# Cross-attention written as steps of one engine each, issued in the order of a table; PSUM as one tensor of three pairs and one of two banks; inverse roots on GpSimd

## The chip, the cores and the metric

One core of a Trainium2 chip runs the whole program as one launch. The metric is device microseconds of that core. The engines are TensorE (PE; its weight loads are listed apart as PEld), VectorE (DVE), ScalarE (ACT), GpSimd (POOL) and SyncE (SP), which here only issues DMAs. Each runs its own instruction queue in order; semaphores tie them together.

## What is computed

Eight batches of 112 tokens of width 256 go through two layers; a context of 375 tokens per batch is shared by both.

```python
# layer 0
n = layernorm(x)
q, k, v = n @ w_q + b_q, ctx @ w_k + b_k, ctx @ w_v + b_v   # 16 heads of 16
x = x + softmax(q k^T / 4) v @ w_out + b_out
n = layernorm(x)                                             # hyperbolic router:
h = project_to_ball(n @ Wp + bp)                             # distance to 8 centroids
x = x + sum over the top 2 experts of share * (gelu(n @ W1 + b1) @ W2 + b2)
# layer 1
n = layernorm(x)
x = x + softmax(q k^T / 4 + mask) v @ Wout                   # no biases, additive mask
n = layernorm(x)
x = x + bit_linear(silu(conv3(bit_linear(n, w1))), w2)       # ternary weights, 8-bit tokens
```

## The kernel before

**Stages.** The program is unrolled. Times are those of the profiled execution: start and first loads (0 to 21 us), attention 0 with the router and the quantisation of the last layer's weights mixed in (to 265), the end of the router (to 293), the experts over 21 tiles of 128 sorted rows with streamed weights (to 453), gathering the experts' rows back (to 474), attention 1 (to 690), the convolutional network (to 769).

**One batch of attention.** `attention()` (L492) holds the steps. `norm` (L529) applies the LN and transposes it (t_n). `query` (L541) makes q (t_q), scaled into two zero-padded copies, with the bias added on DVE in layer 0 (L553). `key` (L561) and `value` (L573) make K (t_k, evicted by ACT) and V (t_v; in layer 0 the bias is added on DVE, L581). `scores` (L587) computes four heads at a time into two PSUM tiles; DVE takes each row's maximum (L602; in layer 1 with the mask added, L608). `lower` (L613) splits the negated maxima in three bf16 parts and transposes them (t_top). `turned` (L627) computes the transposed scores with the maximum subtracted by a second product (L634, L641), in three steps of two tiles each; ACT takes exp (L657), in layer 1 after DVE has added the mask (L652). `weighted` (L663) is p times V (po). `finish_o` (L681), `finish_t` (L695) and `project` (L704) normalise, transpose (t_o, t_oT), project (t_out) and add to x, and take the next LN's statistics.

**Roots.** `ln_stats` (L214) and the router call `rsqrt` (L195): a bit trick and three Newton steps on DVE, ten DVE instructions for an LN's statistics with their bn_stats.

**PSUM.** Three pools: `ps_p` with three tiles of two banks (scores, transposed scores, keys, values), `ps_m` with one bank for all other products, `ps_o` with one bank for po and the router's small products.

**What sets the order.** Each step touches several engines. `add(slot, place, step, ...)` puts it in a plan, four slots to a batch, and L777 calls the steps sorted by slot and place. The Tile scheduler may then move instructions within each engine's queue. It adds the semaphore waits from the tiles that instructions read and write. `late()` (L887) clears the padded buffers and builds the convolution's tap matrices on POOL; it stands after attention 1 in the program, and the scheduler put it at 453 to 458, ahead of the first gathers.

**Loads.** SP issues x of all batches, then ctx of all batches, then wp, w1, w2, the masks and five expert tiles; ACT issues the small columns and layer 0's weights.

Of the kernel before, what the change touches and what calls it, by code (L numbers as in the profile page):

```python
# [21 lines left out]
SK = 375  # L22
# [25 lines left out]
for _name, _w in (("bq", 2), ("bk", 2), ("bp", 2), ("cw", NF * 3), ("cb", NF), ("cent", 2 * E)):  # L48
    COLS[_name] = (_n, _n + _w)
    _n += _w  # L50
NCOLS = _n

NWA, NWB = 2 * F + NF, NF * D + D


@with_exitstack
def xattn_ffn_kernel(
# [21 lines left out]
    xs = [const([S, D], f"x{b}") for b in range(B)]  # L79
    for b in range(B):  # L80
        nc.sync.dma_start(out=xs[b], in_=x_in[b])
    colt = const([128, NCOLS], "cols")
    nc.scalar.dma_start(out=colt, in_=cols)

# [8 lines left out]
    for name, src in (("q", wq0), ("k", wk0), ("v", wv0)):  # L93
        wts[0][name] = load_w(src, f"w{name}0", nc.scalar, f"w{name}")
    ctx_v = ctxT.rearrange("(c p) n -> p c n", p=128)
    ctx_t = []
    for b in range(B):
        t = const([128, 2, SK], f"ctx{b}")
        nc.sync.dma_start(out=t, in_=ctx_v[:, :, b * SK : (b + 1) * SK])
        ctx_t.append(t)  # L100
    rowt = const([128, 2 * D], "rows")
    nc.scalar.dma_start(out=rowt, in_=rows.partition_broadcast(128))
    wts[0]["o"] = load_w(wo0, "wo0", nc.scalar, "wo")
# [55 lines left out]
    topx = [const([S, G, 4, 32], f"top{i}", BF16) for i in range(2)]  # L159
    for t in topx:  # L160
        nc.gpsimd.memset(t, 0.0)
# [5 lines left out]
    nc.gpsimd.memset(minus_magic, -MAGIC)  # L167
    desc = const([128, E], "desc")
# [45 lines left out]
    def ln_stats(b):  # L214

        st = sp.tile([S, 6], F32, tag="bnst", name="bnst")
        nc.vector.bn_stats(st, xs[b])
        mv = sp.tile([S, 2], F32, tag=f"mv{b}", name="mv")
        nc.vector.bn_aggr(mv, st)
        nc.vector.tensor_scalar_add(mv[:, 1:2], mv[:, 1:2], 1e-5)  # L220
        rs = sp.tile([S, 1], F32, tag=f"rs{b}", name="rs")
        rsqrt(mv[:, 1:2], rs, 1, "ln")
        return mv, rs

# [5 lines left out]
    kv = [[None] * B, [None] * B]  # L230
    made = [0]

    def key_buf(layer, b):
        kv[layer][b] = [kp.tile([128, 2, SK], F32, tag="k", name="k"), vbuf[made[0] % 3]]
        made[0] += 1

    def key_products(layer, b, g, t):
        for c in range(2):
            nc.tensor.matmul(  # L239
                t, wts[layer]["k"][:, c, g * 128 : (g + 1) * 128], ctx_t[b][:, c, :],  # L240
                start=(c == 0), stop=(c == 1),
            )

    def value_products(layer, b, i, t):
        for c in range(2):
            nc.tensor.matmul(  # L246
                t, ctx_t[b][:, c, i * KC : (i + 1) * KC], wts[layer]["v"][:, c, :],
                start=(c == 0), stop=(c == 1),
            )
# [5 lines left out]

    class Router:
        def __init__(self, pool, misc, small):
            self.pool, self.misc, self.small = pool, misc, small
            self.cproj = const([128, 2, E], "cproj")
            self.cn = const([128, E], "cn")  # L260
            self.cn1 = const([128, E], "cn1")
# [4 lines left out]
        def ball_scale(self, sq, r, n, name):  # L266

            c = self.tmp(f"c{name}", n, sq.shape[0])
            nc.vector.tensor_scalar_max(c, sq, 1e-14)
            rsqrt(c, r, n, f"ball{name}")  # L270
            nc.vector.tensor_scalar(r, r, 0.95, 1.0, ALU.mult, ALU.min)

        def centroids(self):

            cent = col("cent", 0, 2 * E).rearrange("p (c e) -> p c e", c=2)
            csq = self.pool.tile([128, 2, E], F32, tag="r_csq", name="csq")
            nc.vector.tensor_mul(csq, cent, cent)
            t = self.small("t_c")[:, :E]
            for c in range(2):
                nc.tensor.matmul(t, ones, csq[:, c, :], start=(c == 0), stop=(c == 1))  # L280
            nc.vector.tensor_copy(self.cn, t)
            cs = self.tmp("cs", E, 128)
            self.ball_scale(self.cn, cs, E, "c")
            nc.vector.tensor_mul(self.cproj, cent, cs.unsqueeze(1).to_broadcast([128, 2, E]))
            nc.vector.tensor_mul(self.cn, self.cn, cs)
            nc.vector.tensor_mul(self.cn, self.cn, cs)
            nc.vector.tensor_scalar_min(self.cn, self.cn, 0.99)
            nc.vector.tensor_scalar(self.cn1, self.cn, -1.0, 1.0, ALU.mult, ALU.add)

        def norm(self, b, stats):  # L290
            n = self.pool.tile([S, D], F32, tag="r_n", name="rn")
            ln_apply(n, b, stats)
            return n

        def turn(self, n):
            t = self.misc("t_rn")[:, : 2 * S].rearrange("p (c s) -> p c s", c=2)
            for c in range(2):
                nc.tensor.transpose(t[:, c, :], n[:, c * 128 : (c + 1) * 128], ident[:S, :S])
            nT = self.pool.tile([128, 2, S], F32, tag="r_nT", name="rnT")
            nc.scalar.copy(nT, t)  # L300
            return nT

        def hyper(self, nT):
            t = self.misc("t_xh")[:, : 2 * S].rearrange("p (c s) -> p c s", c=2)
            for o in range(2):
                for c in range(2):
                    nc.tensor.matmul(
                        t[:, o, :], wp_t[:, c, o * 128 : (o + 1) * 128], nT[:, c, :],
                        start=(c == 0), stop=(c == 1),
                    )  # L310
            xh = self.pool.tile([128, 2, S], F32, tag="r_xh", name="xh")
            xsq = self.pool.tile([128, 2, S], F32, tag="r_xsq", name="xsq")
            for o in range(2):
                nc.scalar.activation(xh[:, o, :], t[:, o, :], AF.Identity, bias=col("bp", o))
                nc.scalar.activation(xsq[:, o, :], t[:, o, :], AF.Square, bias=col("bp", o))
            return xh, xsq

        def centre(self, xh, xsq):

            tmp = self.tmp  # L320
            t = self.small("t_g")[:S, : E + 1]
            for c in range(2):
                nc.tensor.matmul(t[:, 0:E], xh[:, c, :], self.cproj[:, c, :], start=(c == 0), stop=(c == 1))
            for c in range(2):
                nc.tensor.matmul(t[:, E : E + 1], xsq[:, c, :], ones[:, 0:1], start=(c == 0), stop=(c == 1))
            g, r = tmp("g", E + 1), tmp("r", 1)
            nc.vector.tensor_copy(g, t)
            self.ball_scale(g[:, E : E + 1], r, 1, "x")
            return g, r

        def distance(self, g, r):

            tmp = self.tmp
            xn = tmp("xn", 1)
            nc.vector.scalar_tensor_tensor(xn, g[:, E : E + 1], r, r, ALU.mult, ALU.mult)
            nc.vector.tensor_scalar_min(xn, xn, 0.99)
            xn1 = tmp("xn1", 1)
            nc.vector.tensor_scalar(xn1, xn, -1.0, 1.0, ALU.mult, ALU.add)
            m2r = tmp("m2r", 1)
            nc.vector.tensor_scalar_mul(m2r, r, -2.0)  # L340

            dif = tmp("dif", E)
            nc.vector.scalar_tensor_tensor(dif, g[:, 0:E], m2r, self.cn[:S], ALU.mult, ALU.add)
            nc.vector.tensor_scalar(dif, dif, xn, 0.0, ALU.add, ALU.max)

            den = tmp("den", E)
            nc.vector.tensor_scalar(den, self.cn1[:S], xn1, 1e-7, ALU.mult, ALU.add)
            nc.vector.reciprocal(den, den)
            nc.vector.scalar_tensor_tensor(dif, dif, 2.0, den, ALU.mult, ALU.mult)
            nc.vector.tensor_scalar(dif, dif, 1.0, 1.0 + 1e-7, ALU.add, ALU.max)  # L350
            v = tmp("v", E)
            nc.vector.tensor_scalar_mul(v, dif, -1.0)
            return v

        def pick(self, v, m, k):

            oh, f = self.tmp(f"oh{k}", E), self.tmp("f", 1)
            nc.vector.tensor_reduce(m[:, k : k + 1], v, AX.X, ALU.max)
            nc.vector.scalar_tensor_tensor(oh, v, m[:, k : k + 1], desc[:S], ALU.is_equal, ALU.mult)
            nc.vector.tensor_reduce(f, oh, AX.X, ALU.max)  # L360
            nc.vector.tensor_scalar(oh, oh, f, None, ALU.is_equal)
            if k == 0:
                nc.vector.scalar_tensor_tensor(v, oh, -1e30, v, ALU.mult, ALU.add)
# [128 lines left out]
    def attention(layer, stats, stats_next):  # L492
        res = None
        with (
# [284 lines left out]
            if layer == 0:  # L779
                res = rt.further()  # L780
# [368 lines left out]
```

## Time and profile before

| what | us |
|---|---|
| times of three runs | 766.53, 777.14, 777.37 (median 777.14) |
| the profiled execution: its time, its span | 771.0, 769.3 |
| mean granted clock of PE in it | 0.872 |
| first scores of attention 0 | 21.31 |
| last output product of attention 0 | 264.35 |
| first expert product | 292.96 |
| first scores of attention 1 | 474.25 |
| last output product of attention 1 | 688.07 |

The profile gives, for each instruction, engine, start and duration; a group is all instructions of one line with the same operands, and "idle before" is the time in which that engine stood before them, with what ended it. The granted clock is PE's clock as a share of full speed. A steady period (from one batch's step to the same step of the next batch) is about 30 us in attention 0 and 27.0 us in attention 1.

### The profile page before, as it was taken

How to read it: one execution, taken by the hardware profiler on the slowest of the kernel's cores; microseconds unless marked ns; L12 is line 12 of the kernel's file. 1: busy time of each engine (PE TensorE's matmuls, PEld its weight loads, DVE VectorE, ACT ScalarE, POOL GpSimd, SP SyncE). 2: the span in 40 equal slices, each digit the busy share in tenths (PEclk: the TensorE clock that was granted, in tenths of full speed). 3: DMA queues.
4: the chain of work that ended last, by engine and by line, in shares of the span. 5: the costliest groups of instructions: out<-in, count | busy, mean ns of one | idle time of the engine just before them, and what ended most of it. 6: DMA issues, size and time to landing. Idle time of an engine off the chain costs nothing.

```text
span 769.3 us, 14093 instructions
## 1 busy us (share of the span) xinstructions
PE 652.8 (85%) x5498; PEld 476.9 (62%) x5498; DVE 415.1 (54%) x1638; ACT 244.6 (32%) x480; POOL 55.8 (7%) x103
## 2 busy tenths in 40 slices
PE   4899889898898738999999984988888888979994
PEld 2455556575566527999889962555555545558883
DVE  6956684856845571011111108777568666775763
ACT  1023332233225203433333420143423332345430
POOL 4000000000000110000000038000000000000000
PEclk9989995988859857999999995589999987879996
DMA  9999101000000103997889902000000000000000
GB/s 297 363 345 350 64 3 60 9 13 29 27 13 8 32 22 128 344 338 279 319 310 355 360 28 78 7 2 1 1 2 2 1 1 2 1 1 1 13 13 24
DMA packets 37070, 81.63 MB, mean 106 GB/s; under 512 B 3228, under 2 KB 30220, under 8 KB 31628
## 3 DMA queue, kind: packets, MB, share of 16 engines
q1 hardware_dynamic: 34092, 75.72, 27.8%
q0 software_dynamic: 1536, 3.67, 1.6%
q10 hardware_dynamic: 1376, 1.34, 0.6%
q8 instruction: 43, 0.70, 0.4%
q14 instruction: 23, 0.19, 0.1%
HBM read 60.54 MB, written 20.19 MB: 105 GB/s over the span
## 4 chain that ended last, share of the span: by engine, by line
PE 39%; DVE 15%; DMA 3%; issue 3%; ACT 1%; POOL 1%; POOLq 0%; DVEq 0%; SPq 0%; ACTq 0%
PE t_h L842 10%; PE t_y L853 9%; PE t_c L1000 4%; DVE sm L608 3%; DVE pT L652 3%; PE sc L597 2%; PE t_v L246 2%; PE t_k L239 2%; PE t_p L634 2%; DMA we<-in_WA_dram 2%; PE po L675 2%; PE t_q L546 1%; PE t_y L1051 1%; DVE a L208 1%; DVE ys L1043 1%
## 5 line engine op out<-in xcount | busy, mean ns | idle before, releaser
L597 PE MATMUL sc<-k,q 32*112 32x375 f32 x512 | 105.1, 599 | 26.5 <-DVE pT L652 15.0
L842 PE MATMUL t_h<-tnT,we 128*128 128x128 f32 x672 | 91.9, 281 | 2.2 <-DMA we<-in_WA_dram 1.9
L842 PEld LDWEIGHTS t_h<-tnT,we 128*128 128x128 f32 x672 | 87.4, 194 | 9.4 <-DVE y L855 2.7
L846 ACT ACTIVATE hT<-t_h,we 128x128 f32<-128x128 f32 x168 | 61.4, 367 | 93.0 <-PE t_h L842 87.5
L634 PE MATMUL t_p<-q,k 32*125 32x224 f32 x768 | 82.0, 426 | 1.2 <-DVE top L602 0.4
L853 PE MATMUL t_y<-we,hT 128*128 128x256 f32 x336 | 82.8, 380 | 0.0
L608 DVE CUSTOM_DVE_ANT_0 sm<-sc,mask 112x375 f32<-112x375 f32 x128 | 62.6, 543 | 34.0 <-PE sc L597 34.0
L602 DVE TENSOR_REDUCE top<-sc 112x2 f32<-112x750 f32 x64 | 58.7, 933 | 32.1 <-PE sc L597 32.0
L657 ACT ACTIVATE pT<-t_p 125x896 f32<-125x896 f32 x48 | 41.4, 914 | 100.1 <-PE t_p L641 100.1
L597 PEld LDWEIGHTS sc<-k,q 32*112 32x112 f32 x512 | 33.9, 198 | 58.5 <-DVE pT L652 25.6
L853 PEld LDWEIGHTS t_y<-we,hT 128*128 128x128 f32 x336 | 59.1, 191 | 5.5
L652 DVE TENSOR_TENSOR pT<-t_p,mask 125x896 f32<-125x896 f32 x48 | 50.1, 1085 | 22.1 <-PE t_p L641 13.7
L657 ACT ACTIVATE pT<-pT 125x896 f32<-125x896 f32 x48 | 45.6, 950 | 51.2 <-DVE pT L652 50.1
L239 PE MATMUL t_k<-ctx,wk 128*128 128x375 f32 x128 | 52.9, 560 | 8.0 <-DMA ctx<-in_ctxT_dram 7.5
L634 PEld LDWEIGHTS t_p<-q,k 32*125 32x125 f32 x768 | 44.9, 209 | 17.4 <-issue 6.1
L675 PE MATMUL po<-pT,v 125*32 125x112 f32 x1536 | 51.5, 283 | 2.7 <-ACT pT L657 2.7
L675 PEld LDWEIGHTS po<-pT,v 125*32 125x32 f32 x1536 | 39.9, 119 | 20.9 <-issue 11.9
L246 PE MATMUL t_v<-wv,ctx 128*125 128x256 f32 x192 | 50.7, 413 | 1.2 <-DVE top L602 1.2
L831 DVE COPY tnT<-t_tn 128x256 f32<-128x256 f32 x21 | 8.9, 425 | 79.0 <-PE t_tn L829 72.5
L855 DVE TENSOR_TENSOR y<-t_y,we 128x256 f32<-128x256 f32 x21 | 8.9, 425 | 68.9 <-PE t_y L853 67.1
L246 PEld LDWEIGHTS t_v<-wv,ctx 128*125 128x125 f32 x192 | 37.8, 205 | 10.2 <-DVE top L602 2.0
L239 PEld LDWEIGHTS t_k<-ctx,wk 128*128 128x128 f32 x128 | 26.7, 222 | 27.3 <-issue 14.4
(214 smaller groups left out, 860.6 us busy)
## 6 DMA issues: line engine op xcount, KB each, us to landing
we<-in_WB_dram SPq DMA_DIRECT2D x21, 1152.0 KB, 7.5
we<-in_WA_dram SPq DMA_DIRECT2D x21, 1028.0 KB, 5.6
tok<-zero SPq DMA_DIRECT2D x8, 896.0 KB, 9.8
ysc<-zero SPq DMA_DIRECT2D x8, 896.0 KB, 10.3
ctx<-in_ctxT_dram SPq DMA_DIRECT2D x8, 375.0 KB, 6.4
tn<-tok SPq DMA_DIRECT2D x21, 128.0 KB, 6.8
ysc<-y SPq DMA_DIRECT2D x21, 128.0 KB, 3.2
we<-in_w1T_dram SPq DMA_DIRECT2D x1, 1024.0 KB, 10.0
```

The costliest lines, as they stand in the source:

```text
L239: nc.tensor.matmul(t, wts[layer]["k"][:, c, g * 128 : (g + 1) * 128], ctx_t[b][:, c, :], start=(c == 0), stop=(c == 1),)
L246: nc.tensor.matmul(t, ctx_t[b][:, c, i * KC : (i + 1) * KC], wts[layer]["v"][:, c, :], start=(c == 0), stop=(c == 1),)
L597: nc.tensor.matmul(ts[j // 2][:S, j % 2, :SK], q[r, c, i, :], k[r, c, :], start=True, stop=True)
L602: nc.vector.tensor_reduce(top[:, g, 2 * m : 2 * m + 2], ts[m][:S, :, :SK], AX.X, ALU.max, negate=True)
L608: nc.vector.tensor_tensor_reduce(out=sm, in0=ts[m][:S, n, :SK], in1=mask_t, scale=-1.0, scalar=3.0e38, op0=ALU.add, op1=ALU.min, accum_out ...
L634: nc.tensor.matmul(ts[j // 2][:KC, j % 2, n * 2 * S : (n + 1) * 2 * S], k[r, c, i * KC : (i + 1) * KC], q[r, c].rearrange("p i s -> p (i s)"),
L652: nc.vector.tensor_tensor(pT, src, mask2[:, lo : lo + 4 * S].unsqueeze(1).to_broadcast([KC, 2, 4 * S]), ALU.add,)
L657: nc.scalar.activation(pT, src, AF.Exp)
L675: nc.tensor.matmul(po[32 * j : 32 * j + 32, g, :], v[:, i, h, :], st[b][f"pT{s}"][r // 2][:, r % 2, lo : lo + S], start=(i == 0), stop=(i ...
L842: nc.tensor.matmul(ph[:, i, :], w1[:, c, f * 128 : (f + 1) * 128], nt[:, c, :], start=(c == 0), stop=(c == 1),)
L846: nc.scalar.activation(hT[:, f, :], ph[:, i, :], AF.Gelu, bias=b1[:, f : f + 1])
L853: nc.tensor.matmul(py, hT[:, f, :], w2[:, f, :], start=(f == 0), stop=(f == NF - 1))
```

## The change

**Steps.** Each step is now what one engine does: the first letter of its name is the engine (P, D, A, G for POOL, S for SP). The main ones: `Pk0, Pk1` and `Pv0..2` (halves of K, thirds of V), their evictions `Aka0, Aka1, Ava0..2`; `Ptn, AnT, Ptq, Aq0, Aq1`; `Ps0..3` with two maxima each (`Dm00` to `Dm31`); `Dsp0..4, Ptt, Alow` (the split maxima); `Pp0..2` with `Da..` (mask, layer 1) and `Ae..` (exp); `Pw0, Pw1` (p times V) with `Au0, Au1`; `Pto, Drc, Do, Pot, AoT, Pout, Dx`; `Dbn, Dba, Grt, Dn` (LN; the names with 2 are those of the next LN). In layer 0 also `Drn, Ptrn, ArnT, Ptxh, Axh, Ptg, Drg, ..., Prank, Drow, ..., Gsc` (router), `Dta..Dtf` (quantisation; `Dtb0` is the second half of the sum over w1), and `PX..` (layer 1's keys and values of batches 0 and 1).

**Order.** `ORDER` gives each step a time, in batches; the step of batch b stands at b + time, and all are issued in the order of these times under a manual schedule, so that nothing is moved within PE, DVE, ACT and POOL.

**PSUM.** One tile `pairs` of three pairs of banks, taken in turn by `Ps` and `Pp`; one tile `banks` of two banks, taken in turn by everything else, K and V among it.

**Engines.** The LN's root, the ball's root and the share's root are `pow` on POOL. q and V are evicted by ACT. The values' bias, which softmax weights that sum to one carry through unchanged, is multiplied by w_out once and added to the output bias. Centroids are normalised once at the start.

**Loads and late work.** wk0 is the first load of the ACT queue, x and ctx of each batch follow one another on SP; the fifth expert tile's load waits for the end of the quantisation of w2. The tap matrices are built one at a time in layer 1 (`Glt0..7`). The experts' and the convolution's code is unchanged.

The core of the diff:

```diff
+ORDER = [
+    [
+        ("Dtb0", -9.7742, 2, 2), ("Dbn", -3.0611, 0, 7), ("Dba", -2.6269, 0, 7), ("Dta0", -1.9080, 2, 2),
+        ("Grt", -1.5529, 0, 7), ("Dta1", -0.9759, 4, 4), ("Dn", -0.6930, 0, 7), ("Ptn", -0.4046, 0, 7),
+        ("AnT", -0.3659, 0, 7), ("Pk0", -0.3527, 0, 7), ("Aka0", -0.2457, 0, 7), ("Ptq", -0.2253, 0, 7),
...
+        ("Ava2", 0.3755, 0, 7), ("Ps0", 0.5977, 0, 7), ("Dm00", 0.6331, 0, 7), ("Dm01", 0.7107, 0, 7),
+        ("Ps1", 0.7235, 0, 7), ("Dm10", 0.7948, 0, 7), ("Sld", 0.9531, 7, 7), ("Dm11", 1.0045, 0, 7),
...
+        ("Dte0", 1.7855, 3, 3), ("Alow", 1.7987, 0, 7), ("Pp0", 1.9159, 0, 7), ("Ae00", 1.9480, 0, 7),
+        ("Ae01", 2.0936, 0, 7), ("Dbv", 2.0991, 0, 0), ("Pp1", 2.2561, 0, 7), ("Ae10", 2.2881, 0, 7),
...
+            pairs = ps.tile([128, 3, 2, 512], F32, tag="pairs", name="pairs")
+            banks = ps.tile([128, 2, 512], F32, tag="banks", name="banks")
+            turn_of = {"pair": 0, "misc": 0}
+
+            def pair(name):
+                turn_of["pair"] += 1
+                return pairs[:, turn_of["pair"] % 3]
+
+            def misc(name):
+                turn_of["misc"] += 1
+                return banks[:, turn_of["misc"] % 2]
...
+                @step(f"Grt{mark}")
+                def _(b, i=i):
+                    rs = sp.tile([S, 1], F32, tag=f"rs{b}", name="rs")
+                    mv = st[b].pop("mv")
+                    nc.gpsimd.tensor_scalar_add(rs, mv[:, 1:2], 1e-5)
+                    nc.gpsimd.tensor_tensor(rs, rs, minus_half[:S, :1], ALU.pow)
...
+            for g in range(G):
+                @step(f"Ps{g}")
+                def _(b, g=g):
+                    q, k = st[b]["q"], kv[layer][b]["k"]
+                    c, i = g // 2, g % 2
+                    st[b][f"s{g}"] = ts = [pair("sc"), pair("sc")]
...
+            plan = sorted((b + t, i, b, n) for i, (n, t, b0, b1) in enumerate(ORDER[layer]) for b in range(b0, b1 + 1))
+            with tc.manual_schedule(engines={ET.PE, ET.DVE, ET.Activation, ET.Pool}):
+                for _, _, b, n in plan:
+                    do[n](b)
```

## The prediction

> **What bounds the kernel now.** I read the page's busy shares and slices first, then busy time by stage, then groups by line, then single rows around the waits.
>
> ```profile
> PE 652.8 (85%) x5498; PEld 476.9 (62%) x5498; DVE 415.1 (54%) x1638; ACT 244.6 (32%) x480; POOL 55.8 (7%) x103
> PEclk9989995988859857999999995589999987879996
> ```
>
> TensorE is busy 85% of the span, and its clock falls now and then. By stage (window, its length, then busy us of PE, PEld, DVE, ACT, POOL, granted clock, DMA share, GB/s):
>
> ```profile
> 21.00:265.00 244.00, 218.32 (x2110) 142.63 (x2110) 157.62 (x646) 73.09 (x131) 15.10 (x17) 0.86 0.29 99
> 265.00:293.00 28.00, 8.76 (x39) 7.09 (x37) 18.78 (x149) 2.24 (x6) 3.77 (x4) 0.57 0.15 45
> 293.00:453.00 160.00, 157.99 (x1046) 144.95 (x1046) 16.84 (x40) 62.71 (x169) 0.00 (x0) 0.99 0.79 291
> 453.00:474.00 21.00, 8.09 (x31) 5.75 (x30) 10.86 (x45) 2.17 (x4) 17.20 (x21) 0.75 0.23 67
> 474.00:690.00 216.00, 187.62 (x1882) 113.81 (x1883) 151.09 (x544) 73.68 (x107) 6.95 (x9) 0.83 0.01 4
> 690.00:769.30 79.30, 62.49 (x361) 55.95 (x359) 45.13 (x101) 28.02 (x60) 3.37 (x6) 0.89 0.04 12
> ```
>
> PE is 89% busy in attention 0 and 87% in attention 1: it bounds both, and DVE has a third of each stage to spare. So work taken off DVE is worth little by itself. What counts is whether PE still finds its next operands and banks ready. The readers of PSUM that release it, and the one wait that costs most in attention 1:
>
> ```profile
> L602 DVE TENSOR_REDUCE top<-sc 112x2 f32<-112x750 f32 x64 | 58.7, 933 | 32.1 <-PE sc L597 32.0
> L657 ACT ACTIVATE pT<-t_p 125x896 f32<-125x896 f32 x48 | 41.4, 914 | 100.1 <-PE t_p L641 100.1
> L608 DVE CUSTOM_DVE_ANT_0 sm<-sc,mask 112x375 f32<-112x375 f32 x128 | 62.6, 543 | 34.0 <-PE sc L597 34.0
> L652 DVE TENSOR_TENSOR pT<-t_p,mask 125x896 f32<-125x896 f32 x48 | 50.1, 1085 | 22.1 <-PE t_p L641 13.7
> ```
>
> ```profile
> 534.68 0.89 PE L597 MATMUL sc<-k,q 32*112 32x375 f32 x4
> 537.75 0.89 PE L597 MATMUL sc<-k,q 32*112 32x375 f32 x4 [2.19 <-DVE pT L652]
> 538.57 2.47 PE L675 MATMUL po<-pT,v 125*32 125x112 f32 x48
> ```
>
> In the second fence PE stands for 2.19 us, and the next step, po, takes 2.47 us where it takes 1.36 at full clock: the slices by half a microsecond show half clock from 538.5 to 542. A hole of 2 us is paid twice.
>
> **The change, part by part.** The order of the compiled program, with its waits, gives more than the diff. `pairs` (six banks) and `banks` (two) are each ONE tensor now, and each access of such a tensor waits for the access before it in program order on another engine, whichever bank that touched. In layer 0 the exp of pair 0 (Ae01) waits for the scores of Ps2, issued after its own products into other banks; the maximum Dm11 of one pair waits for Ae00 of another; Ps1 waits for Dm01, whose pair it does not write. Au0 waits for Ptt, Alow for Ptq, Dx for Ptn, Pv1 for Ava0, Pv2 for AoT. Before, every tile of its pool was a tensor of its own and had only its own readers. So there are two chains per batch, each strictly in the table's order, instead of rings of three and two. I walk one steady period of each layer through these waits, engines in order.
>
> Durations at full clock, from the rows: Ps 0.89, Pp 1.63 (three steps 4.9), Pk 1.40 and Pv 0.95 (t_k 2.79, t_v 2.85 a batch), Pw 1.36, Ptq and Pout 1.12, Ptxh 1.04, Ptg 1.0, Pto 0.65, other transposes 0.4, Prank 0.6; Ae 0.91, Aka 0.57 (layer 0) and 0.43, Ava 0.37, Axh 1.44 (four of 0.36), Aq 0.72 (layer 0), the other ACT copies 0.35 to 0.53; Dm 0.93 in layer 0 and 2x0.54 in layer 1, Da 1.085, Drc and Do 0.25 and 0.42, Dn, Dc, Dbn, Dx 0.42, small DVE operations 0.15 to 0.25. A hop between engines is 0.05, from these rows (DVE ends 470.54, PE starts 470.60 and ends 471.23, ACT starts 471.27):
>
> ```profile
> 470.14 0.40 DVE L227 TENSOR_SCALAR n<-x,mv,rs 112x256 f32<-112x256 f32 x1
> 470.60 0.63 PE L536 MATMUL t_n<-ident,n 112*128 112x112 f32 x2 [11.67 <-DVE n L227]
> 471.27 0.35 ACT L538 COPY nT<-t_n 128x224 f32<-128x224 f32 x1 [11.51 <-PE t_n L536]
> ```
>
> Layer 0, ends of steps from the start of Pp0: Pp0 1.63, Ae00 2.60, Dm11 3.59, Drow 3.76, Ptrn 4.23, ArnT 4.64, Pk1 6.10, Pto 6.75, Aka1 7.38, Ps2 7.64, Ptxh 8.68, Axh 10.18, Drc and Do 10.91, Dm20 (behind them on DVE) 12.00, Pp1 13.69, Ae10 14.66, Dm21 15.65, Ps3 16.60, Ae11 17.57, Dm30 and Dm31 19.66, Pp2 21.35, Pout and Ptn 22.88, Ps0 23.77, Ae21 24.74, AnT 25.09, Pk0 26.55, Pw0 27.91, Ps1 28.80, Ptt 29.16, Au0 29.57, Ptq 30.75, Alow 31.34, Pw1 32.76, then Pp0 again: 33.0 with what is carried over. PE's own bill is 24.0 of it, and it has holes of 1.6, 2.3 and 1.4 us. Period before: 30.
>
> Layer 1, from the start of Ps3: Dm30 and Dm31 3.13, Pp2 4.82, Pk0 6.22, Pv1 7.17, Aka0 7.66, Pot 8.13, Ps0 9.02, Da21 10.17, Dc0 and Dm00 11.68, Ps1 12.63, Dm01 and Dm10 14.87, Pp0 16.56, Dm11, Da00 and Da01 20.07, Ps2 21.02, Pw1 22.38, Pp1 24.01, Dm21, Da10 and Da11 27.34: 27.4. PE's bill is 20.9, the largest hole 2.0. Period before: 27.0.
>
> Half clock on top: I price a hole of over a microsecond at one stretch of 3.5 us like that from 538.5. It loses half its progress over the part of the path that is PE's (16 of 33 us, 12.6 of 27.4; more inside a stretch, where PE's steps are the longer ones: about 0.65), so 1.1 us. Layer 0: three, 3.5 us. Layer 1: the one of 2.0 and a share of five holes of 0.5 to 0.9: 1.8. Bounds: nothing, and half of PE's path at half clock (+8 and +6). Taken: periods 36.5 and 29.2, near the lower bound as the 2.19 us row is.
>
> The sum, against 771.0 (span 769.3; the median shown is 777.1, so I am 6 us under it from the start). Attention 0 lasts 243.0 from first scores (21.31) to its last output product (264.35), 8.1 periods; eight of 36.5 are 292: +49. Attention 1 lasts 213.8, 7.9 periods; eight of 29.2 are 234: +20.
>
> Start: +23. DVE meets the half-sum Dtb0 of w1 before any LN, and w1 lands at 23.1 (issued 13.07, 10.0 to landing). Then Dtb0 1.2, statistics of two batches, a root and Dn: 27.4. Then one chain through `banks`, PE cold as at 12.16 (t_k 4.83): Ptn, AnT 28.7, Pk0, Aka0 32.2, Ptq, Aq 35.8, Pk1, Aka1 38.5, three Pv with their copies 43.5: first scores at 44 instead of 21.3. Bounds +12 (full clock at once) and +26.
>
> Combine, 453 to first scores at 474.25: -9. Taps (3.18) and the hpad memsets (1.3) no longer lead the gathers on POOL; ten DVE operations of an LN become two on DVE; DVE operations of 1.4 and 2.3 us beside POOL work go. Bounds -12, 0.
>
> Roots on POOL (two operations, between a 88 ns memset and an 833 ns tap): hidden by 2 us of slack behind Dba2 in layer 0 and 4 in layer 1; beyond that DVE waits in Drn. DVE loses some 55 us of LN roots, 27 of ball and z roots, 10 of values' bias and 7 of q (24 of 417 ns, 16 of 444): nothing, DVE's time on the path is the maxima, masks and splits, which stay. ACT gains 24 evictions and 32 quarter-q's: they are in the walk. The folded bias (two operations and a product) once: under 2 us. The first loads change places (wk0 first, x and ctx in turns): 0, since the first scores wait for DVE by then. MoE, router tail and FFN: unchanged code, 0, bounds -2 and +4 for the fifth expert load, now behind Dtf1.
>
> 771 + 49 + 20 + 23 - 9 = **854**.
>
> Two rules beside this. The Trainium skill's "PSUM — Partial Sum Buffer", section "PSUM bank collisions raise a hardware error", asks for a guard by bank; by it these chains would not be needed, and the sum would be the first rival's 712. The compiled waits decide. Its "TensorE: Matmul & The Clock Gate", part 1, lets the clock drop after a window of about 3.4 us idle; the 2.19 us row shows a drop after less. By the rule no hole of the walk costs clock, and the sum is 811.
>
> **The rivals.** *The rings hold after all (the other side)*: if waits on other banks' accesses are always met before they matter, PE runs its bill of 24.0 and 20.9 a batch with 11 and 14 us of hops, fill and drain, 203 and 181 us of attention: 771 - 40 - 33 + 14 - 9 - 3 (tail, shorter root chains on DVE) + 12 (the half clock left) = 712. Against it: in the walk such waits end last at some 30 places a period; it decides from periods of 28.5 and 26 (-15 - 6 + 14 - 9 = -16). *No more half clock*: periods 33 and 27.4, 264 and 219: 771 + 21 + 5 + 23 - 9 = 811. For: before ran at 0.86 and 0.83 with holes too. *Clock falls for most of a period*: 41 and 33, 328 and 264: 771 + 85 + 50 + 25 - 9 = 922. For: 115.5 to 136 was half clock with PE busy 18.92 of 20.50 us. *The walk is too strict*: fill and drain are shorter than eight periods and DVE's fewer operations close holes: periods 31 and 27, 248 and 216, start +12: 771 + 5 + 2 + 12 - 9 = 781.
>
> **How the numbers follow.** Chances: the walk with clock 0.42, full clock 0.25, low clock 0.16, too strict 0.11, rings 0.06. Range 780 to 915: from the too-strict case to just under the low-clock case. Faster by over 2% (which is what a measurement here can tell) only with the rings: 0.05. Within 2%: most of the too-strict case, 0.09. Slower: 0.86.
>
> **What would show it.** Right: first scores after 40; maxima and exps of layer 0 that each start just after the other's end, with PE idle before Pk1, Pp1 and Pk0; DVE busy near 105 and 124 us in the two attentions and yet longer stages; PE under 80% busy in both, clock under 0.86 and 0.83. Wrong: PE at 87% or more, periods under 29 and 26. Start, combine and each attention can be read apart.

## The result, and the profile after

The changed kernel takes 816.15 us (median of four runs, 812.27 to 818.54), the kernel before 777.25 (766.53 to 781.77): a ratio of 1.0531, interval 1.0431 to 1.063. Ratios here are of fast runs alone, since some executions of one and the same kernel take some 2% longer at a lower granted clock. The forecast was 854 in a range of 780 to 915. The profiled execution has a span of 816.8 us against 769.3, and its stages show where the 47.5 us arose (ends of stages read from the timeline: first scores, last output product, first expert product, first scores, last output product, end):

| stage | before | after | difference | forecast |
|---|---|---|---|---|
| start to first scores | 21.3 | 46.8 | +25.5 | +23 |
| attention 0 | 244.1 | 265.7 | +21.6 | +49 |
| rest of the router | 27.6 | 40.8 | +13.2 | 0 |
| experts and gathers | 181.3 | 173.3 | -8.0 | -9 |
| attention 1 | 215.9 | 211.2 | -4.7 | +20 |
| convolutional network | 79.2 | 79.0 | -0.2 | 0 |

The busy shares, TensorE's slices and its clock, of the changed kernel:

```profile
PE 621.6 (76%) x5502; PEld 454.3 (56%) x5502; DVE 351.1 (43%) x1096; ACT 269.1 (33%) x576; POOL 95.3 (12%) x185
PE   0587877777777676679999999467777777678994
PEclk9999899979987695879999999668999999788997
```

PE's share fell from 85% to 76%, although the clock is no lower. DVE has 64 us less to do and the kernel is 39 us slower at the median: DVE did not bound it. The two attentions by busy time, with the columns of the windows before:

```profile
46.82:312.48 265.66, 198.63 (x2073) 126.52 (x2072) 113.74 (x369) 91.77 (x185) 32.75 (x50) 0.87 0.16 52
526.62:737.84 211.22, 157.34 (x1902) 98.39 (x1902) 142.36 (x424) 75.12 (x134) 26.96 (x45) 0.90 0.02 7
```

No engine is busy more than 75% of either stage. That is the mark of waits, and the groups by line name them. The maxima of layer 0, the scores, and the exp:

```profile
L796 DVE TENSOR_REDUCE topf<-pairs 112x2 f32<-112x750 f32 x64 | 59.3, 935 | 107.8 <-ACT pT L869 70.8
L786 PE MATMUL pairs<-k,q 32*112 32x375 f32 x512 | 66.6, 594 | 33.8 <-DVE pT L857 18.1
L869 ACT ACTIVATE pT<-pairs 125x896 f32<-125x896 f32 x48 | 43.9, 920 | 68.3 <-PE pairs L846 34.5
```

Before, the maxima stood 32.1 us in front of this line, all of it for scores, which are their data. Now DVE stands 107.8 us, of which 70.8 for an exp on ACT. A maximum uses nothing of an exp: it waits because the exp touched another pair of the same tensor just before it in the program. In the timeline, around one Pp0 of attention 0:

```profile
223.28 0.66 PE L839 MATMUL pairs<-q,k 32*125 32x224 f32 x8
225.17 0.36 PE L454 MATMUL banks<-ind,below 112*112 112x8 f32 x2 [0.65 <-ACT q L728]
227.02 0.41 PE L334 MATMUL banks<-ident,rn 112*128 112x112 f32 x2 [1.29 <-DVE row L461]
227.87 2.51 PE L740 MATMUL banks<-ctx,wk 128*128 128x375 f32 x4 [0.44 <-ACT rnT L339]
235.39 2.04 PE L760 MATMUL banks<-wv,ctx 128*125 128x256 f32 x4 [2.02 <-DVE dif L420]
```

```profile
224.99 0.94 ACT L869 ACTIVATE pT<-pairs 125x896 f32<-125x896 f32 x1
```

```profile
225.96 0.94 DVE L796 TENSOR_REDUCE topf<-pairs 112x2 f32<-112x750 f32 x1 [4.75 <-ACT pT L869]
226.81 0.15 DVE L461 TENSOR_TENSOR row<-banks,first 112x8 f32<-112x8 f32 x1
```

Read across the engines: Ae00 ends at 225.93 and Dm11 starts at 225.96, Drow follows it on DVE and ends at 226.96, Ptrn starts on PE at 227.02. These are the walk's links in the walk's order, 0.03 to 0.06 us apart, with the holes where the walk had them (1.29 for the 1.6 before Ptrn, 2.02 for the 2.3 before Pv0). Pk1, at 227.87, takes 2.51 us instead of the walk's 1.40: it fell into a stretch at half clock.

### The profile page after: what moved, and what is told of

Same layout as the page of the kernel before. It is cut to its first block, busy times and chain, and to the rows that moved or that the text cites. A ratio compares the mean times of both kernels' runs of the same rounds, so it can differ in the third digit from the quotient of the medians.

```text
span 816.8 us, 13738 instructions
## 1 busy us (share of the span) xinstructions
PE 621.6 (76%) x5502; PEld 454.3 (56%) x5502; DVE 351.1 (43%) x1096; ACT 269.1 (33%) x576; POOL 95.3 (12%) x185
## 4 chain that ended last, share of the span: by engine, by line
PE 61%; DVE 20%; ACT 8%; DMA 6%; issue 4%; POOL 1%; ACTq 0%; SPq 0%; POOLq 0%; DVEq 0%
PE t_h L1049 9%; PE t_y L1060 8%; PE pairs L786 8%; PE pairs L839 6%; PE banks L740 5%; DVE pT L857 5%; DVE sm L802 5%; PE banks L884 4%; DVE topf L796 4%; PE t_c L1204 4%; ACT pT L869 3%; PE banks L760 3%; PE banks L933 2%; DMA tok<-rn,at 2%; PE banks L713 1%
## 5 line engine op out<-in xcount | busy, mean ns | idle before, releaser
L796 DVE TENSOR_REDUCE topf<-pairs 112x2 f32<-112x750 f32 x64 | 59.3, 935 | 107.8 <-ACT pT L869 70.8
L786 PE MATMUL pairs<-k,q 32*112 32x375 f32 x512 | 66.6, 594 | 33.8 <-DVE pT L857 18.1
L839 PE MATMUL pairs<-q,k 32*125 32x224 f32 x768 | 62.8, 417 | 25.6 <-DVE topf L802 13.0
L802 DVE CUSTOM_DVE_ANT_0 sm<-pairs,mask 112x375 f32<-112x375 f32 x128 | 63.7, 544 | 39.7 <-PE pairs L786 27.9
L740 PE MATMUL banks<-ctx,wk 128*128 128x375 f32 x128 | 62.5, 621 | 15.1 <-ACT nT L705 7.1
L760 PE MATMUL banks<-wv,ctx 128*125 128x256 f32 x192 | 59.9, 443 | 16.7 <-DVE dif L420 6.1
L869 ACT ACTIVATE pT<-pairs 125x896 f32<-125x896 f32 x48 | 43.9, 920 | 68.3 <-PE pairs L846 34.5
L857 DVE TENSOR_TENSOR pT<-pairs,mask 125x896 f32<-125x896 f32 x48 | 50.5, 1082 | 21.1 <-PE pairs L786 13.4
L839 PEld LDWEIGHTS pairs<-q,k 32*125 32x125 f32 x768 | 33.8, 205 | 40.6 <-DVE topf L802 19.1
L884 PE MATMUL banks<-pT,v 125*32 125x112 f32 x1536 | 47.8, 277 | 7.6 <-ACT low L828 5.5
L1204 PE MATMUL t_c<-hpad,taps 128*128 128x224 f32 x192 | 40.8, 362 | 1.9 <-DVE hpad L1195 1.9
```

The costliest lines, as they stand in the source:

```text
L740: nc.tensor.matmul(t, wts[lay]["k"][:, c, o * 128 : (o + 1) * 128], ctx_t[batch(b)][:, c, :], start=(c == 0), stop=(c == 1),)
L760: nc.tensor.matmul(t, ctx_t[batch(b)][:, c, i * KC : (i + 1) * KC], wts[lay]["v"][:, c, :], start=(c == 0), stop=(c == 1),)
L786: nc.tensor.matmul(ts[j // 2][:S, j % 2, :SK], q[r, c, i, :], k[r, c, :], start=True, stop=True)
L796: nc.vector.tensor_reduce(top[:, g, 2 * m : 2 * m + 2], t[:S, :, :SK], AX.X, ALU.max, negate=True)
L802: nc.vector.tensor_tensor_reduce(out=sm, in0=t[:S, n, :SK], in1=mask_t, scale=-1.0, scalar=3.0e38, op0=ALU.add, op1=ALU.min, accum_out=top ...
L839: nc.tensor.matmul(ts[j // 2][:KC, j % 2, n * 2 * S : (n + 1) * 2 * S], k[r, c, i * KC : (i + 1) * KC], q[r, c].rearrange("p i s -> p (i s)"),
```

## The experiments

### Tiles of their own

The chain theory says that the slowdown is the two tensors. Its rival says that it is the fixed order of steps, with the work moved to ACT. The first experiment takes the tensors apart and leaves everything else. Two more do this for one of them:

```diff
-            pairs = ps.tile([128, 3, 2, 512], F32, tag="pairs", name="pairs")
-            banks = ps.tile([128, 2, 512], F32, tag="banks", name="banks")
+            pairs = [ps.tile([128, 2, 512], F32, tag=f"pair{i}", name=f"pair{i}") for i in range(3)]
+            banks = [ps.tile([128, 512], F32, tag=f"bank{i}", name=f"bank{i}") for i in range(2)]
...
-                return pairs[:, turn_of["pair"] % 3]
+                return pairs[turn_of["pair"] % 3]
...
-                return banks[:, turn_of["misc"] % 2]
+                return banks[turn_of["misc"] % 2]
```

Expected of both, of the pairs alone, and of the banks alone:

> The changed kernel with three tiles of a pair of banks and two tiles of one bank in place of one tensor each; same steps, same order, same engines, only the waits follow each buffer's own readers. Chain theory (waits on accesses to other banks of the tensor make the changed kernel slower): attention 0 from 265.7 to about 212 us (PE's bill of 24.0 a batch plus hops), attention 1 from 211.2 to about 190, the tail behind attention 0 from 40.8 to about 30: 816 becomes about 731. Rival (the fixed order of steps and the work moved to ACT cost the time, whatever the tiles): within 10 us of the changed kernel, 806 to 820.

> Only the pairs get tiles of their own; the two banks stay one tensor. Chain theory: the chain through the two banks in attention 0 is 24.3 us of products and readers a batch before hops, with 8.5 us of the pairs' products on PE between them, so a period of 28 to 30: attention 0 about 235, attention 1 about 200, the tail unchanged near 40: about 775. Rival (order and engines): 806 to 820.

> Only the two banks get tiles of their own; the three pairs stay one tensor. Chain theory: the pairs' chain is 23.4 us a batch in attention 0 and 25 in attention 1, so attention 0 about 225, attention 1 about 205 (nearly unchanged), the tail near 30: about 760. Rival (order and engines): 806 to 820.

| kernel | median us | ratio to before, interval | start | attention 0 | router | experts, gathers | attention 1 |
|---|---|---|---|---|---|---|---|
| changed | 816.15 | 1.0531, 1.0431 to 1.063 | 46.8 | 265.7 | 40.8 | 173.3 | 211.2 |
| pairs their own | 748.64 | 0.9704, 0.9609 to 0.9798 | 46.8 | 229.3 | 44.0 | 175.1 | 175.9 |
| banks their own | 734.30 | 0.9543, 0.9457 to 0.9629 | 34.6 | 208.5 | 31.3 | 173.3 | 203.7 |
| both | 643.52 | 0.8349, 0.8276 to 0.8421 | 34.5 | 165.8 | 33.7 | 173.2 | 157.4 |

The rival is out: with the same steps, order and engines the kernel loses 173 us and takes 0.835 of the kernel before. Either chain's removal alone brings 67 and 82 us; the other 23 come only with both gone. The banks' chain alone makes 12 us of the start and about 10 of the router's end; the pairs' chain makes most of attention 1 (35 of 54 us). The two attentions with both apart, and the maxima and exps of that kernel:

```profile
34.50:200.26 165.76, 162.36 (x2075) 111.54 (x2074) 112.19 (x369) 89.82 (x186) 32.76 (x50) 1.00 0.32 107
407.14:564.56 157.42, 151.05 (x1902) 98.25 (x1902) 140.61 (x423) 73.01 (x133) 26.70 (x45) 0.93 0.03 9
```

```profile
L796 DVE TENSOR_REDUCE topf<-pair 112x2 f32<-112x750 f32 x64 | 58.9, 934 | 32.3 <-PE pair L786 32.1
```

```profile
L869 ACT ACTIVATE pT<-pair 125x896 f32<-125x896 f32 x48 | 43.3, 919 | 18.9 <-PE pair L846 18.1
```

PE is busy 98% and 96% of the two stages, the maxima wait for scores again and for little else, and attention 0 runs at full clock throughout. Each expectation named too little: the forecasts for attention 0 of 212, 235 and 225 us came out at 165.8, 229.3 and 208.5. Of the 100 us by which attention 0 is shorter than in the changed kernel, 63.6 are idle time of PE (67.0 to 3.4) and 36.3 busy time for the same products, at a granted clock of 1.00 in place of 0.87. And the maxima's wait for the exp goes with the pairs: with only the banks taken apart it is still 59.1 us, with only the pairs taken apart it is gone.

### The chain put into the kernel before

```diff
-            tc.tile_pool(name=f"ps_p{layer}", bufs=3, space=PSUM) as ps_p,
+            tc.tile_pool(name=f"ps_p{layer}", bufs=1, space=PSUM) as ps_p,
...
+            pairs = ps_p.tile([128, 3, 2, 512], F32, tag="p", name="pairs")
+            pair_of = [0]
...
             def pair(name):
-                return ps_p.tile([128, 2, 512], F32, tag="p", name=name)
+                pair_of[0] += 1
+                return pairs[:, pair_of[0] % 3]
```

> The kernel before with its three pairs of banks as one tensor in place of three tiles; nothing else is changed. Chain theory: attention 0 from 244 to about 265 and attention 1 from 216 to about 230 us, 771 becomes about 805. If the scheduler orders around the waits or they are met before they matter: within 10 us of the kernel before.

Measured: 940.03 us, ratio 1.2147 (1.2021 to 1.2272). Attention 0 takes 314.2 us in place of 244.1, attention 1 312.4 in place of 215.9. The two attentions:

```profile
23.40:337.57 314.17, 232.28 (x2095) 149.11 (x2096) 162.62 (x634) 71.83 (x130) 15.09 (x17) 0.77 0.22 74
546.28:858.69 312.41, 215.87 (x1882) 128.65 (x1883) 159.00 (x544) 74.96 (x106) 6.87 (x8) 0.66 0.01 3
```

So the chain needs nothing else of the change to cost time, and the scheduler does not order around it: it costs this kernel 162 us by the medians of these runs (778.11 before), five times what I expected. PE is busy longer for the same work, at a granted clock of 0.77 and 0.66 in place of 0.86 and 0.83. (Keys and values share the pairs in this kernel, so its chain is longer than the changed kernel's.)

### The order of the table

The version with tiles of its own, without the manual schedule:

```diff
-            with tc.manual_schedule(engines={ET.PE, ET.DVE, ET.Activation, ET.Pool}):
+            if True:
```

> Tiles of their own, but the order within the engines' queues left to the scheduler instead of held to the table. If the waits were all and the table's order is worth nothing by itself: 635 to 660. If the table's order is what keeps PE fed (the rival to the chain theory, as a gain): back towards the kernel before, 700 to 770, with PE idle in attention 0 again.

Measured: 695.85 us, 0.9002 (0.8887 to 0.9116): 52 us above the same steps in the table's order, neither of the two forecasts (4 us below the second). The stages of the profiled execution, which is 44 us above that of the same steps in the table's order: start 22.6, attention 0 209.7, router 28.7, experts and gathers 185.6, attention 1 163.5. The order is worth 44 us in attention 0 and 6 in attention 1, 12 between the experts and the first scores, and costs 12 us at the start (the sum Dtb0) and 5 at the router's end. So with tiles of their own the order is a gain of its own. What it is worth under the chains was not tried, and which other parts of the change make this kernel 10% faster than the one before, even in the scheduler's order, was not taken apart.

### The start

```diff
-        ("Dtb0", -9.7742, 2, 2),
+        ("Dtb0", -0.9000, 2, 2),
```

In the changed kernel, and with tiles of their own:

> The changed kernel with the half-sum Dtb0 of w1 issued after the first layer norms instead of before them. If the wait for w1 at the head of DVE's queue sets the start: first scores 12 us earlier than 46.8, total about 804. If the chain of bank steps at half clock alone sets it, or x and the weights come no earlier: within 3 us of the changed kernel.

> Tiles of their own (643.5 us) and the half-sum Dtb0 after the first layer norms. If the two costs of the start and of the chains are separate, the 11.2 us that the later sum gave alone come on top: first scores near 22 instead of 34.5, total about 632. If the sum then falls where DVE is wanted: 638 to 644.

Measured: 804.98 us (1.0441, 1.0349 to 1.0532), 11 us under the changed kernel, with first scores at 32.0; and 636.92 us (0.8221, 0.8139 to 0.8304), the fastest here, with first scores at 25.4 in place of 34.5; the total lies between the two forecasts. The two causes of the late start overlap: without the wait for w1 it is 14.8 us earlier, without the chain of `banks` 12.3, without both 21.4. In the changed kernel:

```profile
26.90 0.60 PE L700 MATMUL banks<-ident,n 112*128 112x112 f32 x2 [19.77 <-DVE mv L673]
27.94 2.87 PE L740 MATMUL banks<-ctx,wk 128*128 128x375 f32 x4 [0.43 <-ACT nT L705]
31.48 2.05 PE L713 MATMUL banks<-nT,wq 128*128 128x112 f32 x8 [0.66 <-ACT k L751]
35.07 2.87 PE L740 MATMUL banks<-ctx,wk 128*128 128x375 f32 x4 [1.54 <-ACT q L728]
38.60 2.07 PE L760 MATMUL banks<-wv,ctx 128*125 128x256 f32 x4 [0.66 <-ACT k L751]
```

The walk had AnT done at 28.7, the copies of q at 35.8 and Pk1's at 38.5: each came within a microsecond. The three Pv with their copies, 5.0 us in the walk, took 7.7. Every product waits for the copy of the one before it, and all run at half speed (four products of t_k in 2.87 us, 1.53 later). The 9 that the page shows as clock in these slices does not speak against it: the trace has no record of the clock before 50.8 us, and a stretch without a record counts as full clock.

### The roots

On DVE again, by Newton steps, in three kernels: with tiles of their own, in the changed kernel, and the reverse edit (pow on GpSimd) in the kernel before.

```diff
-                    nc.gpsimd.tensor_scalar_add(rs, mv[:, 1:2], 1e-5)
-                    nc.gpsimd.tensor_tensor(rs, rs, minus_half[:S, :1], ALU.pow)
+                    nc.vector.tensor_scalar_add(mv[:, 1:2], mv[:, 1:2], 1e-5)
+                    rsqrt(mv[:, 1:2], rs, 1, "ln")
```

> Tiles of their own, with the layer norms' roots by Newton steps on DVE again (some 1.4 us of DVE for each of 32 in place of two GpSimd operations of 0.26 and 0.58 us). If DVE's relief is worth nothing, as the prediction had it: attention 0 (DVE busy 112 of 166 us) unchanged, attention 1 (141 of 157 us) up to 8 us longer: 644 to 652. If DVE bounds the steps once PE is fed: 660 to 690.

> The changed kernel, its two tensors kept, with the layer norms' roots by Newton steps on DVE. With tiles of their own the same edit cost 33 us. If DVE's relief is hidden while the chains bound (the prediction's nothing): 812 to 822. If the Newton steps fall between links of the chains, since DVE runs in order: 830 to 850.

> The kernel before with the layer norms' roots as pow on GpSimd, nothing else changed. Prediction's view (DVE's relief is worth nothing where PE bounds): within 8 us of the kernel before. If DVE's order already held PE up there, as it does with tiles of their own: 740 to 760.

Measured: 676.39 us with tiles of their own (0.874, 0.8652 to 0.8828, against 0.8349): 33 us longer. In the changed kernel 1.0719 (1.0604 to 1.0834) against 1.0531: about 15 us longer; the two intervals overlap a little, the times compared do not (828.74 to 839.58 against 812.27 to 818.54). In the kernel before 769.48 us (0.9959, 0.9907 to 1.0012): no difference. So the same relief is worth nothing, some 15 and 33 us. With tiles of their own and Newton steps, the two attentions:

```profile
36.40:211.66 175.26, 165.69 (x2074) 113.78 (x2074) 131.25 (x489) 90.23 (x186) 21.95 (x28) 0.98 0.29 97
420.14:588.77 168.63, 158.06 (x1902) 100.41 (x1902) 151.38 (x512) 73.56 (x134) 12.51 (x15) 0.93 0.03 8
```

Beside the lines of the kernel without them: DVE gains 19 and 11 us of work, and the stages grow by 9.5 and 11.2. DVE still has 44 us to spare in attention 0, and the stage grows by half of what DVE gained even so. In the trace PE's idle time there grows from 3.4 to 9.6 us. It is spread over waits for DVE results of several kinds, the router's `row`, `su`, `rn` and `g` and the sum x (1 to 2.2 us each, two of them there before), with only 0.8 for a maximum; and 6.8 us run at half clock, where there were none. In attention 1 the idle time grows by 4.2 us; the waits that grow most are those for masked scores (0.4 to 2.4), for a copy on ACT (0.5 to 2.3) and for the first operation of the root itself (none to 1.6). The other 7.0 us are longer busy time of PE, for the most part unexplained. I read it as the ten short instructions delaying whatever stands behind them in a fixed queue; no single link carries the price. Beyond the attentions, the start and the gathers take 1.9 us each. These differences are of the profiled executions, which lie 25 us apart; the medians lie 33 apart.

### The taps

All eight tap matrices and the clearing of the buffers ahead of the first gathers, in the fastest version: the eight entries `Glt0` to `Glt7` of the table get the time -1.5 of batch 0.

> The best version so far (636.9 us) with all eight tap matrices and the clearing of the padded buffers issued on GpSimd ahead of the first gathers. The prediction's price: gathers start later by 8 x 0.85 + 1.3 = 8 us less the 1.7 us that one tap and nothing else cost there before: total about 643 to 645. If the gathers wait for the experts' last rows anyway: 636 to 638.

Measured: 639.30 us (0.8228, 0.8158 to 0.8298) against 636.92, which is no clear difference; in the profiled executions the first gather starts 8.3 us behind the experts' last product instead of 3.2, and the stage of experts and gathers is 177.0 us against 173.5. That lies between the two forecasts. In the kernel before, taps and gathers:

```profile
453.55 1.32 POOL L889 MEMSET hpad<- 128x456 f32 x3 [165.81 <-DVE y L855]
454.83 3.18 POOL L891 TENSOR_TENSOR taps<-ident,cols 128x384 f32<-128x384 f32 x4
458.17 0.99 POOL L522 DMA_INDIRECT yg<-ysc,at  x1 [0.15 <-issue]
```

and in the changed kernel:

```profile
515.88 0.96 POOL L652 DMA_INDIRECT yg<-ysc,at  x1 [167.69 <-issue]
```

The experts' last product ends at 453.0 before and at 512.7 after, so the first gather starts 5.2 and 3.2 us behind it. Taking 4.5 us of work from in front of the gathers brought 2.0. The other 3.2 us stay with nothing else on POOL; the last rows are issued at 513.18, and I take the gathers to wait for their landing, which no row shows.

## Why the prediction was right or wrong

**The bound, and the direction: right.** PE's share fell and the holes are where the walk put them. The cause that the prediction named, accesses chained across one tensor's banks, is shown by the three kernels with tiles of their own and by the chain put into the kernel before. Of the signs named in advance, late first scores, links one after the other and a PE under 80% busy came out. Others did not: attention 1 is not longer, the clock in the attentions, 0.87 and 0.90, is not under 0.86 and 0.83, and a period under 26, named as a sign of being wrong, is what attention 1 has. DVE was busy 113.7 and 142.4 us where I had 105 and 124.

**The period of attention 0: the walk's 33.0 lies near the measured 34 by luck, and the stage was too long.** Prank of three successive batches starts at 191.39, 225.17 and 259.42: 33.8 and 34.3. But these are not periods at full clock. From 151.56 to 254.10, three periods, the granted clock is 0.85, 0.90 and 0.85, which is 7 to 10 us at half clock in each; the forecast had three stretches of 3.5. The same four products of Pk1 at full and at half clock:

```profile
158.35 1.53 PE L740 MATMUL banks<-ctx,wk 128*128 128x375 f32 x4 [0.63 <-ACT rnT L339]
194.00 2.77 PE L740 MATMUL banks<-ctx,wk 128*128 128x375 f32 x4 [0.43 <-ACT rnT L339]
```

With Pto behind it, that stretch cost 1.65 us. Two of them in a period of 33.9 make about 3 us, so that some 31 are left at full clock; this is an estimate from these rows. So the half clock's 3.5 us was about right here, and the walk at full clock was some 2 us too long: Pp at 1.63 us was a mean with half clock in it, where its rows at full clock show 1.24. Half clock was counted twice, in the durations and on top: 36.5 instead of 34. I also took eight such periods. Ptt of the eight batches starts 27.3, 27.4, 30.6, 34.0, 33.9, 34.7 and 30.4 us apart; the first output product stands at 112.36 and the first of the router at 126.71, so the early batches have less to do. The stage is 27 us shorter than forecast.

**The half-clock term failed in attention 1.** I priced each hole of over a microsecond at a stretch of 3.5 us, from one row of the kernel before, and took 1.8 us a period. In attention 1 the stretches at half clock add up to 44 us, 72 before, and none of them lies between 559.4 and 699.3: the clock stays full through one hole of 2.05 us and one of 1.66 us in each of the following periods:

```profile
577.54 0.90 PE L786 MATMUL pairs<-k,q 32*112 32x375 f32 x8 [2.05 <-DVE pT L857]
578.37 1.36 PE L884 MATMUL banks<-pT,v 125*32 125x112 f32 x48
```

The scores and po after such a hole take 0.90 and 1.36 us, where po took 2.47 after the hole of 2.19 in the kernel before. So the length of a hole does not decide by itself; its place does too. The clock changes only in steps of 3.41 us. In the kernel before, the hole of 2.19 lies whole in the step that ends at 538.58, and PE is busy 1.22 us of that step. The hole of 2.05 here is split over two steps, with PE busy 2.32 and 2.30 us. The next one that lies whole in a step, 2.14 us ending at 698.61, is followed by half clock at 699.31. The Trainium skill's "TensorE: Matmul & The Clock Gate", section "Part 1: The HAM clock gate", has the clock fall after an idle window of about 3.4 us. The length of the step agrees; but the idle time did not have to fill it, and the measurement decides. The rival without this term, 811, was the nearest, in part by luck: its two attentions come to +26 us where +17 was measured, and it too had nothing for the router.

**The period of attention 1: mis-sized.** Forecast 27.4 and 29.2 with half clock, measured 24.7:

```profile
592.31 0.37 PE L821 MATMUL banks<-ident,top 112*128 112x112 bf16 x4
617.02 0.37 PE L821 MATMUL banks<-ident,top 112*128 112x112 bf16 x4
641.81 0.37 PE L821 MATMUL banks<-ident,top 112*128 112x112 bf16 x4
```

Besides the half clock, the step that failed is Pp at 1.63 us, a third of 4.9 us a batch; at full clock three such steps take about 1.24 us each, which is 1.2 us a period less. The rest is 0.1 to 0.2 us at each of the other links of the pairs' chain. Without half clock on top this made -4.7 us where I had +20.

**The end of the router: wrong, 0 in place of +13.2.** "Unchanged code" was true of the router and not of what stands between its steps: the table puts the keys and values of attention 1 for two batches there, and with one tensor for both banks they alternate with the last batch's router. The banks with tiles of their own bring the stage from 40.8 to 31.3 us, the pairs do not (44.0). So 7 to 10 of the 13 us are that chain (33.7 with both apart), and the keys and values themselves cost no more than the rest. This miss went the other way than those of the attentions, which were 52 us too high together: without it the forecast of 854 would have been further off.

**The start: right,** +23 against +25.5, and both its parts were shown apart; the missing 2.5 us are the three Pv at half speed.

**Gathers to first scores: right in size, half wrong in cause.** -9 against -8.0, but the taps are 2.0 of it. The larger part, 5.5 us, is DVE's: the first batch's x is complete at 462.7 before and its norm starts at 470.14, behind other batches' statistics and gathered rows; after, 520.4 and 522.33. How much of it is the order and how much the shorter root was not taken apart; Newton steps put back cost this stage 1.9 us with tiles of their own.

**Roots at nothing: wrong as a rule.** It held in the kernel before. In the changed kernel the same roots on DVE cost some 15 us, with tiles of their own 33. The prediction looked at DVE's busy time, not at what stands behind the instructions in its queue.

**The first rival's price was wrong as well.** I had 712 for rings that hold; tiles of their own give 643.5. PE's bill of 24.0 and 20.9 us a batch carried half clock in its durations, and I kept 12 us more of it. Kept busy, PE does a batch in 20.7 us of attention 0 and 19.7 of attention 1 (still at a clock of 0.93), the layer's time by eight.

## What to carry to other kernels

Before reading a ring of buffers in the source as a ring, read the waits of the compiled program: buffers cut from one tensor may be handed on one access at a time, across engines and in program order, and giving each its own tile can be worth more than the rest of a rewrite (here 816 to 643.5 us). A relief of an engine that is not the bound is priced by what stands behind it in its queue, not by its busy share, and again after the bound has moved. Take durations for a walk from rows at the clock that the walk assumes; a mean that has half clock in it counts the half clock twice when it is put on top.

## What the runs showed of the hardware

A pow on GpSimd took 0.58 us for 112x1 and 0.81 us for 112x2 elements, in groups of 32 and 8 (0.68 for 112x1 in another group of 8):

```profile
L680 POOL TENSOR_TENSOR rs<-rs,mhalf 112x1 f32<-112x1 f32 x32 | 18.4, 576 | 2.7
L496 POOL TENSOR_TENSOR q<-z,phalf 112x2 f32<-112x2 f32 x8 | 6.4, 806 | 0.0
```

In all thirteen traces the clock changes in steps of 3.41 us, between full and half. Each of the 117 steps at full clock in which PE idled over 1.9 us, in one hole or several, was followed by half clock; of the 1916 that were followed by full clock none had more than 1.89. Another 97 with less idle time were followed by half clock too, so something besides idle time counts, and what that is stays open.

The granted clock did not simply follow PE's busy share: it was 1.00 in attention 0 with tiles of their own (PE busy 98%), 0.86 in the kernel before (89%), 0.77 with the chain put into it (74%); but 0.90 in attention 1 of the changed kernel (74%) against 0.83 before (87%).
